# Mamba's softplus sums: from GpSimd additions to TensorE products with the identity

## The chip, the cores and the metric

The kernel runs on one core of one Trainium2 chip. The metric is the device time of one execution in microseconds (us). The core has five engines with a queue each: TensorE (matmuls, PE in the profile, its weight loads PEld), VectorE (DVE), ScalarE (ACT), GpSimd (POOL) and SyncE (SP), which here only issues transfers.

## The reference, cut to what matters

The network has four layers: two Mamba blocks, a convolution that makes local attention weights, linear attention with a mixture of experts, and softmax attention with a second mixture of experts. The change touches the Mamba blocks alone, all in float32, on 2 images of 1024 tokens with 256 channels (512 inside a block, 16 states):

```python
xs = jax.nn.silu(jnp.transpose(xc, (0, 2, 1)))          # after in_w and a causal convolution of 4 taps
x_dbl = xs @ xproj_w
dt, Bm, Cm = jnp.split(x_dbl, [DT_RANK, DT_RANK + D_STATE], axis=-1)
delta = jax.nn.softplus(dt @ dt_w + dt_b)
A = -jnp.exp(A_log)
dA = jnp.exp(delta[..., None] * A)
dBu = delta[..., None] * Bm[:, :, None, :] * xs[..., None]
def step(hst, ins):
    dA_t, dBu_t, C_t = ins
    hst = dA_t * hst + dBu_t
    y_t = jnp.einsum('bdn,bn->bd', hst, C_t)
    return (hst, y_t)
...
y = jnp.swapaxes(ys, 0, 1) + xs * Dp
y = y * jax.nn.silu(res)
out = y @ out_w + out_b
```

The kernel computes softplus(z) as max(z, 0) + ln(1 + e) with e = exp(-|z|). It corrects the logarithm for the rounding of 1 + e: with w = (1 + e) - 1 as rounded, it adds e - w. So delta is a sum of four terms, max(z, 0) + e + ln(1 + e) - w.

## The kernel before, in words

**Units.** Each Mamba block works through its 2048 tokens in 4 chunks of 512, so there are 8 units of one block and one chunk. The inner 512 channels are 4 parts of 128 (index dc), one channel to a partition, tokens along the free dimension. `layer0` (L575) runs the units one after the other. A unit has a front (`Mamba.front`, L293), a scan (`Mamba.scan`, L415) and a back (`Mamba.back`, L485).

**Front.** It makes xs (input projection L309, evicted by ScalarE at L313; convolution as 4 accumulating matmuls with diagonal matrices L336, evicted at L342; SiLU L345), then the small projection (L351), C transposed (L364), and z (L380). ScalarE takes from z's PSUM tile |z| into e (L385) and max(z, 0) into delta (L389), and runs exp (L393) and ln (L396) over all four parts at once. The tile e lies in the buffer tagged pre, which the next front's pre needs, and ln lies in the buffer tagged gate, which the back's gate needs (each tag has one buffer). Then for each of the four parts:

```python
nc.scalar.activation(w, e[:, dc, :], AF.Identity, bias=net.one)   # L403
nc.scalar.activation(w, w, AF.Identity, bias=net.minus_one)       # L404
eng.tensor_sub(w, e[:, dc, :], w)                                 # L405
eng.tensor_add(ln[:, dc, :], ln[:, dc, :], w)                     # L407
eng.tensor_add(delta[:, dc, :], delta[:, dc, :], ln[:, dc, :])    # L409
eng.tensor_mul(w, delta[:, dc, :], xs[:, dc, :])                  # L411, w is du
```

with a `yield` after each of the last four. The engine `eng` is GpSimd in seven units. The first unit's front runs alone, with no scan beside it (alone=True): there eng is VectorE, VectorE also does max(z, 0) (L387) and w (L401, one instruction), and exp and ln run part by part.

**Scan.** For each of 16 states n: a transfer spreads B's row over the partitions, GpSimd makes h = du * B for two parts at a time (L461; VectorE in the first state of the first unit), and for each of the 4 parts ScalarE makes da = exp(delta * A) in PSUM (L468, 3 buffers) and VectorE runs the recurrence (L472). So a unit has 64 scan steps. After each step two things advance by one: the work on the state before (TensorE transposes h for 128 tokens in four 128x128 pieces, L440, into one of 3 PSUM buffers; one step later VectorE multiplies by C and adds to ya, L449, or ScalarE does it for two of the states, L447), and `paced` (L552).

**Order of the work.** `paced` deals out generator steps over the 63 slots behind those scan steps by a table in `layer0`: for each generator a number of steps, a first slot and a last. Of the next unit's front, 22 steps (HEAD) go to slots 0 to 38, and 16 steps to slots 38 to 62. These 16 are the four yields of the four parts above. Beside them the back of the unit before has 9 steps in slots 0 to 35 (gate projection L494, evicted by ScalarE at L498 and put through SiLU at L502; y as L507 and transposes back L512, multiplied by the gate at L516) and 7 in slots 40 to 61 (output projection L524 and L528, layer norm L150 to L168, transposes L179, L540, and GpSimd's residual additions L543 and L548). The making of the next layer's taps (`Taps.make`: transposes L700, copies L702, matmuls L706, copies L711) has 9 steps, 12 in the first unit, in slots 40 to 63. All these matmuls share the two PSUM buffers tagged mm. Each engine runs its queue in order; the queues are laid down when the program is built and need not follow the order of the code.

**Diagonals.** GpSimd makes the convolution's diagonal matrices from the identity (L269), 128x128 each, before the first unit and again for the second block in slots 26 to 38 of the third.

Of the kernel before, what the change touches and what calls it, by code (L numbers as in the profile page):

```python
# [10 lines left out]
F32 = mybir.dt.float32  # L11
# [8 lines left out]
P = 128  # L20
# [7 lines left out]
TC = 512  # L28
# [205 lines left out]
class Mamba:  # L234
# [58 lines left out]
    def front(self, j, alone=False):  # L293


        net, nc, m, one, two = self.net, self.net.nc, self.m, self.one, self.two
        eng = nc.vector if alone else nc.gpsimd
# [3 lines left out]
        xs = two.tile([P, NDC, TC], F32, tag="xs", name=f"{m}_xs_{j}", bufs=3)  # L301
# [4 lines left out]
        for mc in range(NDC):  # L306
            ps = self.ps_mm.tile([P, TC], F32, tag="mm", name=f"{m}_in_{j}_{mc}")
            for kc in range(NCC):
                nc.tensor.matmul(  # L309
                    ps, lhsT=self.in_sb[:, kc, mc * P : (mc + 1) * P], rhs=self.xt[:, kc, tok],  # L310
                    start=(kc == 0), stop=(kc == NCC - 1),
# [8 lines left out]
        for dc in range(NDC):  # L320
            b = net.col(f"{m}_conv_b", dc)
# [12 lines left out]
            ps = self.ps_mm.tile([P, TC], F32, tag="mm", name=f"{m}_conv_{j}_{dc}")  # L334
            for k in range(4):
                nc.tensor.matmul(  # L336
                    ps, lhsT=self.taps[:, dc * 4 + k, :], rhs=pre[:, dc, k : k + TC],
                    start=(k == 0), stop=(k == 3),
# [10 lines left out]
        ps = self.ps_mm.tile([P, TC], F32, tag="mm", name=f"{m}_xd_ps_{j}")  # L349
        for dc in range(NDC):  # L350
            nc.tensor.matmul(  # L351
                ps[:XD, :], lhsT=self.xp_sb[:, dc, :], rhs=xs[:, dc, :],
                start=(dc == 0), stop=(dc == NDC - 1),
# [8 lines left out]
        ps = self.ps_mm.tile([P, TC], F32, tag="mm", name=f"{m}_ct_ps_{j}")  # L362
# [10 lines left out]
        delta = two.tile([P, NDC, TC], F32, tag="delta", name=f"{m}_delta_{j}")  # L373
        e = one.tile([P, NDC, 3 + TC], F32, tag="pre", name=f"{m}_e_{j}")[:, :, :TC]
        ln = one.tile([P, NDC, TC], F32, tag="gate", name=f"{m}_ln_{j}")
        du = two.tile([P, NDC, TC], F32, tag="du", name=f"{m}_du_{j}")
        for dc in range(NDC):
            pool, tag = (self.ps_ht, "ht") if alone and dc else (self.ps_mm, "mm")
            ps = pool.tile([P, TC], F32, tag=tag, name=f"{m}_dt_{j}_{dc}")
            nc.tensor.matmul(  # L380
                ps, lhsT=self.dt_sb[:, dc * P : (dc + 1) * P], rhs=xd[:RANK, :],
                start=True, stop=True,
            )
            b = net.col(f"{m}_dt_b", dc)
# [6 lines left out]
        parts = [slice(dc, dc + 1) for dc in range(NDC)] if alone else [slice(0, NDC)]  # L391
# [6 lines left out]
        for dc in range(NDC):  # L398
            w = du[:, dc, :]
            if alone:  # L400
                nc.vector.tensor_scalar(w, e[:, dc, :], 1.0, -1.0, ALU.add, ALU.add)  # L401
            else:
                nc.scalar.activation(w, e[:, dc, :], AF.Identity, bias=net.one)  # L403
                nc.scalar.activation(w, w, AF.Identity, bias=net.minus_one)  # L404
            eng.tensor_sub(w, e[:, dc, :], w)  # L405
            yield
            eng.tensor_add(ln[:, dc, :], ln[:, dc, :], w)  # L407
            yield
            eng.tensor_add(delta[:, dc, :], delta[:, dc, :], ln[:, dc, :])  # L409
            yield  # L410
            eng.tensor_mul(w, delta[:, dc, :], xs[:, dc, :])  # L411
            yield
        self.chunks[j] = xs, bd, ct, delta, du

# [137 lines left out]
def paced(n, parts):  # L552

    taken = [0] * len(parts)
    for slot in range(n):
        for i, (steps, many, first, end) in enumerate(parts):
            while taken[i] < many and slot >= first + (end - first) * taken[i] / many:
                next(steps, None)
                taken[i] += 1
        yield  # L560
    for steps, *_ in parts:
        for _ in steps:
            pass


def both(a, b, n):

    for i, _ in enumerate(a):
        if i % n == n - 1:
            next(b, None)  # L570
    for _ in b:
        pass


def layer0(net, x, x_dram, m1, m2, load_image, taps, conv_dram, lg):  # L575

    tc, nc = net.tc, net.nc  # L580
    with (
        tc.tile_pool(name="m_w", bufs=1) as wpool,
        tc.tile_pool(name="m_one", bufs=1) as one,
        tc.tile_pool(name="m_two", bufs=2) as two,
        tc.tile_pool(name="m_scan", bufs=2) as scanp,
        tc.tile_pool(name="m_dram", bufs=2, space=DRAM) as dram,
        tc.tile_pool(name="m_mm", bufs=2, space=PSUM) as ps_mm,
        tc.tile_pool(name="m_ht", bufs=3, space=PSUM) as ps_ht,
        ExitStack() as last,
    ):  # L590
        ps_da = last.enter_context(tc.tile_pool(name="m_da", bufs=3, space=PSUM))
        xt = x.rearrange("p c b t -> p c (b t)")
        pools = (wpool, one, two, scanp, dram, ps_mm, ps_da, ps_ht)
        blocks = [
            Mamba(net, "m1", pools, xt, None, *m1), Mamba(net, "m2", pools, xt, x_dram, *m2)
        ]
        norm = GroupNorm(net, wpool, ps_ht, x)
        blocks[0].load()
        for _ in blocks[0].diagonals():
            pass  # L600
        load_image()
        for _ in blocks[0].load_rest():
            pass
        rows = net.first_rows(wpool, ["m1_out_b", "m2_out_b"])
        for m, r in zip(blocks, rows):
            m.out_b = r
        norm.image(0)
        units = [(m, j) for m in blocks for j in range(NCH)]
        norm.image(1)
        for _ in units[0][0].front(0, alone=True):  # L610
            pass
        before, done = iter(()), []
        aside = taps.make(ps_mm, conv_dram)
        for u, (m, j) in enumerate(units):
            steps = [(b, Mamba.GATED, 0, 35) for b in done]
            fronts = []
            for a, k in units[u + 1 : u + 2]:
                if k == 0:
                    a.load()
                fronts.append(a.front(k))  # L620
            if u == NCH - 2:

                steps.append((blocks[1].diagonals(), NDC * 4, 26, 38))
            rest = m.load_rest() if u and j == 0 else iter(())
            steps += [(f, Mamba.HEAD, 0, 38) for f in fronts]
            steps += [(rest, 1, 37, 38)]
            steps += [(f, 16, 38, 62) for f in fronts] + [(b, 7, 40, 61) for b in done]
            steps += [(rest, 1, 62, 63)]
            if u + 1 < len(units):
                n = 9 if u else 12  # L630
                steps += [(islice(aside, n), n, 40, 63)]
            else:
                last.close()
                m.ps_da = last.enter_context(tc.tile_pool(name="m_da2", bufs=2, space=PSUM))
                ps_acc = last.enter_context(tc.tile_pool(name="m_acc", bufs=1, space=PSUM))

                def place(u):
                    pool, tag, w = {
                        3: (one, "pre", TC + 3), 0: (two, "xs", TC), 1: (two, "delta", TC),
                        2: (two, "du", TC),  # L640
                    }[u]
                    a = pool.tile(
                        [P, NDC, w], F32, tag=tag, name=f"early_{u}",
                        bufs=3 if tag == "xs" else None,
                    )
                    return taps.load(u, a.rearrange("p d t -> p (d t)"))

                pair = {u: place(u) for u in taps.ORDER}
                acc = {0: taps.bank(ps_acc.tile([P, TC], F32, tag="acc", name="early_acc"))}
                steps += [(taps.convolve(0, pair, acc), 56, 3, 63)]  # L650
            before = m.scan(j, before, paced(63, steps), u == 0)
            done = [m.back(j)]
        taps.read(acc, lg)
        for _ in before:
            pass
        acc = {
            k: taps.bank(ps_ht.tile([P, TC], F32, tag="ht", name=f"early_acc{k}")) for k in (1, 2)
        }
        both(taps.convolve(0, pair, acc), done[0], 3)
        taps.read(acc, lg)  # L660
# [945 lines left out]
def conv_attn_hybrid(ctx: ExitStack, tc: tile.TileContext, a: dict, out: bass.AP):  # L1606
# [6 lines left out]
    with tc.tile_pool(name="conv_w", bufs=2) as convw:  # L1613
        def load_x(b):
            for cc in range(NCC):
                nc.sync.dma_start(x[:, cc, b, :], a["x"][b, cc])

        load_x(0)
        taps = Taps(net, convw, main, x, a["l1_w1"], a["l1_w2"])
        layer0(  # L1620
            net, x, a["x"],
            [a[f"m1_{k}"] for k in ("in_w", "out_w", "xproj_w", "dt_w")],
            [a[f"m2_{k}"] for k in ("in_w", "out_w", "xproj_w", "dt_w")],
            lambda: load_x(1), taps, conv_dram, lg,
        )
# [117 lines left out]
```

## Time and profile before

| | us |
|---|---|
| runs of the kernel before | 2184.31, 2189.04, 2190.55 (median 2189.04) |
| the profiled execution's own time | 2188.29 |
| its span, first to last instruction | 2186.6 |
| Mamba stage, first scan to last scan | 53.3 to 1031 |
| TensorE busy, whole span | 1894.0 |
| VectorE busy, whole span | 1400.3 |
| GpSimd busy, whole span | 1028.9 |
| ScalarE busy, whole span | 959.2 |
| L405, L407, L409 on GpSimd, 28 of each | 33.2, 35.6, 35.6 |
| L472, 512 scans on VectorE | 318.7 + 303.3 |
| L449, 448 multiply-adds on VectorE | 320.2 |
| L461, 254 products on GpSimd | 594.5 |

How to read it: a view by stretch gives for each engine the time in which it was busy within a window. A view of waits gives, for an engine that stood idle, the instruction that then ran, the one whose end released it, and the sum, count and longest of such waits. In lines of groups the numbers after the count are busy time, mean ns of one, and idle time of the engine just before them with its releasers. In a timeline the columns are start, duration, engine, line, operation, tiles, shape and count, and in brackets the idle time before and its releaser; instructions of one kind that follow each other are one line. A float32 matmul appears as two MATMUL records, a transpose as one. A busy TensorE is not TensorE at its peak, since matmuls overlap and their ends are modelled. PEclk is the share of its full clock that TensorE was granted.

### The profile page before, as it was taken

What the parts mean: (1) busy time and instruction counts of PE and PEld (TensorE: products, weight loads), DVE (VectorE), ACT (ScalarE), POOL (GpSimd) and SP (SyncE); (2) the same over time, 40 slices, a digit from 0 to 9 for tenths busy, and PEclk for the clock granted to TensorE, in tenths of its full rate; (3) what the DMA queues carried; (4) which work ended last, traced back from release to release, by engine and by line L of the source; (5) the groups of instructions that cost most, each with busy time, mean ns of one, the idle gap of its engine ahead of it and who ended that gap; (6) DMA issues with size and microseconds to landing.
All of it is one profiled execution on the core that took longest, in us unless ns stands there. A gap on an engine that the chain in (4) does not pass through costs nothing.

```text
span 2186.6 us, 27311 instructions
## 1 busy us (share of the span) xinstructions
PE 1894.0 (87%) x9652; PEld 1335.5 (61%) x9652; DVE 1400.3 (64%) x2210; ACT 959.2 (44%) x1610; POOL 1028.9 (47%) x726
## 2 busy tenths in 40 slices
PE   6888898898978888788999989949999599859996
PEld 2464555556555655454646556539999467649995
DVE  6999998999999999899005475752222544432223
ACT  4676677767777767645013454411111132301111
POOL 3796787959698686965025420012332000023331
PEclk9869889898989889899999999969999799979997
DMA  2121121111212111310030100028998200059997
GB/s 106 45 68 39 37 69 35 58 35 45 62 47 60 38 49 35 85 42 17 0 64 1 48 15 10 20 82 306 326 329 323 82 10 10 20 206 327 329 323 292
DMA packets 90499, 223.87 MB, mean 102 GB/s; under 512 B 35467, under 2 KB 51728, under 8 KB 79732
## 3 DMA queue, kind: packets, MB, share of 16 engines
q1 hardware_dynamic: 77636, 198.29, 27.1%
q0 software_dynamic: 7728, 19.15, 2.9%
q10 hardware_dynamic: 4992, 4.59, 0.7%
q8 instruction: 81, 1.33, 0.3%
q14 instruction: 62, 0.51, 0.1%
HBM read 204.60 MB, written 19.37 MB: 102 GB/s over the span
## 4 chain that ended last, share of the span: by engine, by line
PE 32%; DVE 22%; issue 19%; POOL 11%; ACT 10%; DMA 5%; POOLq 0%; SPq 0%; DVEq 0%; ACTq 0%
DVE m_h L472 11%; DVE m_ya L449 6%; PE acc L762 3%; POOL x L1520 3%; POOL l_yd L1570 3%; PE m_ht L440 3%; PE early_acc L762 3%; PE av L1276 3%; ACT m_da L468 2%; PE sc L1250 2%; DMA l_yd<-y,target 2%; POOL m_h L461 2%; PE h L1099 2%; PE m_xd_ps L351 1%; PE w L1108 1%
## 5 line engine op out<-in xcount | busy, mean ns | idle before, releaser
L461 POOL TENSOR_TENSOR m_h<-m_du,m_b 128x1024 f32<-128x1024 f32 x254 | 594.5, 2364 | 196.0 <-PE m_ht L440 95.8
L440 PE MATMUL m_ht<-ident,m_h 128*128 128x128 f32 x2048 | 361.2, 305 | 119.4 <-DVE m_ya L449 83.9
L440 PEld LDWEIGHTS m_ht<-ident,m_h 128*128 128x128 f32 x2048 | 259.5, 154 | 317.8 <-DVE m_ya L449 112.7
L468 ACT ACTIVATE m_da<-m_delta,m_aneg 128x512 f32<-128x512 f32 x512 | 349.5, 690 | 220.8 <-DVE m_h L472 220.1
L1520 POOL DMA_INDIRECT x<-l_zd,source x82 | 84.8, 1034 | 573.1 <-DVE source L1465 217.1
L449 DVE SCALAR_TENSOR_TENSOR m_ya<-m_ht,m_ct,m_ya 128x512 f32<-128x512 f32 x448 | 320.2, 733 | 18.4 <-PE m_ht L440 17.5
L472 DVE TENSOR_TENSOR_SCAN m_h<-m_da,m_state,m_h 128x512 f32<-128x512 f32 x256 | 318.7, 1271 | 14.7 <-POOL m_h L461 8.7
L472 DVE TENSOR_TENSOR_SCAN m_h<-m_da,m_h 128x512 f32<-128x512 f32 x256 | 303.3, 1210 | 23.6 <-ACT m_da L468 13.1
L1550 PEld LDWEIGHTS h<-xts,we 128*128 128x128 f32 x2528 | 298.4, 194 | 7.1 <-issue 3.4
L1550 PE MATMUL h<-xts,we 128*128 128x128 f32 x2528 | 299.4, 277 | 2.2 <-issue 1.7
L1557 DVE TENSOR_TENSOR hid<-hid,h 128x512 f32<-128x512 f32 x79 | 54.3, 688 | 258.9 <-PE h L1550 258.9
L1556 ACT ACTIVATE hid<-h 128x512 f32<-128x512 f32 x79 | 47.2, 598 | 384.6 <-issue 324.0
L1564 PE MATMUL o<-we,hid 128*128 128x256 f32 x632 | 150.4, 380 | 2.2 <-DVE y L1569 1.6
L1570 POOL DMA_INDIRECT l_yd<-y,target x79 | 79.3, 1003 | 142.6 <-DVE y L1569 136.3
L1564 PEld LDWEIGHTS o<-we,hid 128*128 128x128 f32 x632 | 113.7, 190 | 15.7 <-DVE y L1569 2.8
L336 PE MATMUL m_conv<-m_pre,m_taps 128*128 128x512 f32 x240 | 114.6, 596 | 6.7 <-ACT m_gate L498 5.6
L762 PE MATMUL early_acc<-x,early 128*98 128x448 f32 (+21 forms) x308 | 97.0, 447 | 0.0
L762 PE MATMUL acc<-x,pair 128*98 128x416 f32 (+21 forms) x308 | 93.6, 452 | 0.0
L1569 DVE COPY y<-o 128x256 f32<-128x256 f32 x79 | 33.6, 425 | 69.6 <-PE o L1564 69.6
L309 PE MATMUL m_in<-x,m_in_sb 128*128 128x512 f32 x128 | 68.8, 663 | 9.8 <-ACT m_pre L313 6.9
L762 PEld LDWEIGHTS acc<-x,pair 128*98 128x98 f32 x308 | 47.7, 167 | 39.9 <-issue 34.5
L528 PE MATMUL m_out<-m_out_sb,m_xs 128*128 128x256 f32 x256 | 68.7, 397 | 0.0
(318 smaller groups left out, 2843.3 us busy)
## 6 DMA issues: line engine op xcount, KB each, us to landing
we<-in_l_experts_dram SPq DMA_DIRECT2D x82, 1536.0 KB
m_b<-m_bd SPq DMA_DIRECT2D x128, 256.0 KB
w<-in_l_w_dram SPq DMA_DIRECT2D x21, 256.0 KB
l_zd<-l_z SPq DMA_DIRECT2D x7, 512.0 KB
l_yl<-l_yd SPq DMA_DIRECT2D x10, 256.0 KB
l_yl<-l_yd ACTq DMA_DIRECT2D x10, 256.0 KB
early<-taps SPq DMA_DIRECT2D x7, 343.0 KB
pair<-taps SPq DMA_DIRECT2D x7, 343.0 KB
```

Source lines behind the costliest of these rows:

```text
L309: nc.tensor.matmul(ps, lhsT=self.in_sb[:, kc, mc * P : (mc + 1) * P], rhs=self.xt[:, kc, tok], start=(kc == 0), stop=(kc == NCC - 1),)
L336: nc.tensor.matmul(ps, lhsT=self.taps[:, dc * 4 + k, :], rhs=pre[:, dc, k : k + TC], start=(k == 0), stop=(k == 3),)
L440: nc.tensor.transpose(ps[:, dc * P : (dc + 1) * P], hs[dc // G][:, dc % G, i * P : (i + 1) * P], net.ident,)
L449: nc.vector.scalar_tensor_tensor(ya[:, i, :], ps, c, ya[:, i, :], ALU.mult, ALU.add)
L461: (nc.vector if start and n == 0 else nc.gpsimd).tensor_mul(h, du[:, g * G : (g + 1) * G, :], b.unsqueeze(1).to_broadcast(half))
L468: nc.scalar.activation(da, delta[:, dc, :], AF.Exp, scale=self.aneg[:, i : i + 1])
L472: nc.vector.tensor_tensor_scan(h, da, h, 0.0 if first else state[:, n, dc : dc + 1], ALU.mult, ALU.add)
L762: nc.tensor.matmul(a[:, lo - 16 * k : hi - 16 * k, co : co + n], lhsT=lhsT, rhs=self.x[:, kc, b, lo - r0 : hi - r0, ci : ci + n], start=(u ...
L1520: nc.gpsimd.indirect_dma_start(out=x, out_offset=None, in_=zd[:, :], in_offset=bass.IndirectOffsetOnAxis(ap=source[:, g : g + 1], axis=0), ...
L1550: nc.tensor.matmul(ps[:, at], lhsT=w12[:, s, kc, at], rhs=xt[:, kc * P : (kc + 1) * P], start=(kc == 0), stop=(kc == NCC - 1),)
L1564: nc.tensor.matmul(ps[:, :C], lhsT=ht[:, mc * P : (mc + 1) * P], rhs=w[:, 8 + mc, :], start=(mc == 0), stop=(mc == NHC - 1),)
L1570: nc.gpsimd.indirect_dma_start(out=yd[g], out_offset=bass.IndirectOffsetOnAxis(ap=target[:, g : g + 1], axis=0), in_=y, in_offset=None, bo ...
```

## The change

In each part, the three additions and subtractions (L405, L407, L409) give way to four accumulating matmuls: delta, e and ln each times the identity, and du (which holds w) times a new matrix, minus the identity. ScalarE copies the sum from PSUM to delta. The product with xs (L411) stays on eng; in the first unit's front it reads the sum from PSUM, elsewhere from delta. The sum lies in a buffer tagged mm; in the first unit's front the odd parts take one tagged ht. The yields of a part fall from four to three, and the table in `layer0` gives the front's second portion 12 steps in place of 16, over the same slots. GpSimd makes minus the identity once, ahead of the first unit.

```diff
@@ front, the loop over the four parts
             else:
                 nc.scalar.activation(w, e[:, dc, :], AF.Identity, bias=net.one)
                 nc.scalar.activation(w, w, AF.Identity, bias=net.minus_one)
-            eng.tensor_sub(w, e[:, dc, :], w)
-            yield
-            eng.tensor_add(ln[:, dc, :], ln[:, dc, :], w)
-            yield
-            eng.tensor_add(delta[:, dc, :], delta[:, dc, :], ln[:, dc, :])
-            yield
-            eng.tensor_mul(w, delta[:, dc, :], xs[:, dc, :])
+            yield
+
+            pool, tag = (self.ps_ht, "ht") if alone and dc % 2 else (self.ps_mm, "mm")
+            ps = pool.tile([P, TC], F32, tag=tag, name=f"{m}_sp_{j}_{dc}")
+            parts = (net.ident, delta), (net.ident, e), (net.ident, ln), (net.minus, du)
+            for k, (i, a) in enumerate(parts):
+                nc.tensor.matmul(
+                    ps, lhsT=i, rhs=a[:, dc, :], start=(k == 0), stop=(k == len(parts) - 1)
+                )
+            nc.scalar.copy(delta[:, dc, :], ps)
+            yield
+            eng.tensor_mul(w, ps if alone else delta[:, dc, :], xs[:, dc, :])
             yield
@@ layer0, before the units
+        net.minus = wpool.tile([P, P], F32, name="minus_ident")
+        nc.gpsimd.tensor_scalar_mul(net.minus, net.ident, -1.0)
@@ layer0, the table of a unit
-            steps += [(f, 16, 38, 62) for f in fronts] + [(b, 7, 40, 61) for b in done]
+            steps += [(f, 12, 38, 62) for f in fronts] + [(b, 7, 40, 61) for b in done]
```

## The prediction

> **What bounds the kernel now.** I read the busy time by stretch first. Counting 64 scans (L472) to a unit, a unit of the Mamba stage has an early part (scans 0 to 37, beside the next unit's projections) and a late part (38 to 63, where the softplus sums lie). Units 3 and 4, late, late and early, with the late part of unit 0 ahead:
>
> ```profile
> core 0: us, PE busy (x) PEld busy (x) DVE busy (x) ACT busy (x) POOL busy (x), PEclk, DMA share, GB/s
> 118.60:165.30 46.70, 39.92 (x180) 29.51 (x181) 43.91 (x49) 34.12 (x70) 45.30 (x29) 0.67 0.25 71
> 487.80:543.20 55.40, 44.63 (x231) 33.92 (x231) 50.25 (x63) 42.19 (x64) 50.10 (x31) 0.81 0.13 44
> 610.30:664.40 54.10, 42.43 (x230) 31.81 (x230) 49.63 (x65) 43.84 (x79) 50.69 (x33) 0.84 0.16 53
> 543.20:610.30 67.10, 62.22 (x286) 36.17 (x284) 65.19 (x74) 48.54 (x85) 48.30 (x24) 1.00 0.19 57
> ```
>
> VectorE is the bound: 97% busy early, 91% late, and its work is untouched by the change in seven of eight units. So at most its idle time can be won: 3 to 6 us in each late part, 33 us over seven (375.6 us of late parts less 342.8 busy). GpSimd is as busy as VectorE in the late part only; that is where its sums are. TensorE's clock is low there. Next, who VectorE waits for, from 118 to 914 us (us, times, longest):
>
> ```profile
> DVE m_h L472 <- ACT m_da L468: 19.0, 23, 2.5
> DVE m_h L472 <- POOL m_h L461: 17.3, 11, 4.9
> DVE m_ya L449 <- PE m_ht L440: 15.9, 22, 2.2
> ```
>
> Of the 17.3, the timeline puts 6.1 behind the tap diagonals of L269 and 2.7 behind residual adds and a DMA near 800 us; neither is touched. The other 8.5 lie at 165, 412, 419, 536, 664, 782 and 907 us: ends of late parts, or the first scan after one. GpSimd had lost its lead. Around 905 us, GpSimd and then ScalarE:
>
> ```profile
> 904.57 2.35 POOL L461 TENSOR_TENSOR m_h<-m_du,m_b 128x1024 f32<-128x1024 f32 x1
> 906.87 1.27 POOL L407 TENSOR_TENSOR m_ln<-m_ln,m_du 128x512 f32<-128x512 f32 x1
> 908.70 1.28 POOL L409 TENSOR_TENSOR m_delta<-m_delta,m_ln 128x512 f32<-128x512 f32 x1
> ```
> ```profile
> 910.01 0.69 ACT L498 ACTIVATE m_gate<-m_g,cols_sb 128x512 f32<-128x512 f32 x1 [6.57 <-POOL m_delta L409]
> ```
>
> The gate shares its buffer with ln, so ScalarE stood 6.57 us until GpSimd had added ln, and the exponentials (L468) behind it came late: VectorE lost 2.5 us at 911 and, the same way, 1.4 at 163.
>
> **What the Trainium skill says.** "Perfetto Trace Analysis", Identifying the Most-Contended Engine: matmul busy time does not measure headroom. The trace agrees: of the 44.63 us at 487.8, counted start to start at full clock (0.109 us for 128 columns, 0.216 for 256, 0.43 for 512), the records hold about 31 us, so TensorE has some 24 us to spare. "TensorE: Matmul & The Clock Gate", What's actually happening: an idle array runs at half clock until it has been busy for about a window of 3.4 us. The trace agrees: eight records in the time of four,
>
> ```profile
> 29.45 3.63 PE L351 MATMUL m_xd_ps<-m_xs,m_xp_sb 128*48 128x512 f32 x8
> ```
> ```profile
> 211.84 3.46 PE L351 MATMUL m_xd_ps<-m_xs,m_xp_sb 128*48 128x512 f32 x4
> ```
>
> and PEclk 0.67 to 0.84 late against 1.00 early. "SBUF — State Buffer", Who interferes with whom: a VectorE instruction with at most one SBUF input does not contend with GpSimd. The trace agrees: scans wholly under a GpSimd product took 1239 ns, scans beside none 1240. So fewer GpSimd instructions make no VectorE instruction of the scan faster.
>
> **The change, part by part.** Durations from groups by form:
>
> ```profile
> L405 POOL TENSOR_TENSOR m_du<-m_e,m_du 128x512 f32<-128x512 f32 x28 | 33.2, 1184 | 0.0
> L407 POOL TENSOR_TENSOR m_ln<-m_ln,m_du 128x512 f32<-128x512 f32 x28 | 35.6, 1273 | 1.1
> L409 POOL TENSOR_TENSOR m_delta<-m_delta,m_ln 128x512 f32<-128x512 f32 x28 | 35.6, 1271 | 1.5
> L336 PE MATMUL m_conv<-m_pre,m_taps 128*128 128x512 f32 x240 | 114.6, 596 | 6.7 <-ACT m_gate L498 5.6 <-ACT m_pre L313 1.1
> L702 ACT COPY w1ts<-w1t 128x512 f32<-128x512 f32 x21 | 12.3, 584 | 4.5 <-PE w1t L700 4.1 <-ACT m_state L432 0.2
> ```
>
> *Removed:* 84 GpSimd instructions, 33.2 + 35.6 + 35.6 = 104 us, 14.9 a unit: GpSimd falls from 50 to 35 us of a 54 us late part and keeps its lead. Worth the 8.5 us above; I add 1.5 of the 2.7 at 800 and the 1.9 just after 914, where adds fell on a lead already spent. Gain 10, bounds 8.5 and 13.1. *Moved:* ln is now released by TensorE, which does not queue behind products: the 2.5 + 1.4 = 3.9 us go.
>
> *Added, TensorE:* four matmuls a part. L336's 120 matmuls show as 240 records, two each, so 8 records x 0.43 = 3.44 us in one uninterrupted piece (6.9 at half clock), 13.8 a unit. 31 + 13.8 = 45 of 54 us: it fits. It also keeps the clock up: some 5 us of the 19.0 are late exponentials behind the tap copies, which wait for slow products late in the part (clock half from 519 to 536, 639 to 656, 765 to 782). I take half, 2.5; bounds 0 and 8 (with part of the m_ht waits). *Added, ScalarE:* 28 copies x 0.58 = 16 us, 2.3 a unit on 42 of 54 busy: hidden by its waits for scans. If that cover were gone, 16 us.
>
> *Added wait:* the copy waits for its four matmuls. Queued behind it are the exponentials that VectorE's next scans need, with three PSUM buffers of lead (one is used in 1.8 us: scan 1.14 and m_ya 0.64). GpSimd's product L411 waits for the copy, with the products of L461 behind it, but has 15 us of slack. The queues do not follow the program's order (at the start L405 runs at 38.5 us, before three earlier L387), so where a copy stands can't be read off the code. Bounds: below, what late hand-overs cost now, 5 us over some 66 in units 1 to 6, 0.07 each; above, a burst that outlasts the lead at half clock, 6.9 - 5.4 = 1.5. It can't be a gain, since it only adds a wait. The nearest bursts, L507 and L512 of the early part (0.86 + 16 x 0.11 = 2.6 us, four a unit), go with 1.7 us of waits in m_ht and 0.3 at L516 a unit, at most 0.5 each. I take 0.25: 28 x 0.25 = 7 us. Steps of the sums go from 16 to 12 over the same 24 slots, still six slots a part: nothing.
>
> *The first unit's front* runs alone, on VectorE, and is in the chain:
>
> ```profile
> 51.53 1.22 DVE L461 TENSOR_TENSOR m_h<-m_du,m_b 128x1024 f32<-128x1024 f32 x1
> 52.66 0.69 DVE L411 TENSOR_TENSOR m_du<-m_delta,m_xs 128x512 f32<-128x512 f32 x1
> 54.40 2.40 DVE L461 TENSOR_TENSOR m_h<-m_du,m_b 128x1024 f32<-128x1024 f32 x1
> 56.72 7.90 DVE L472 TENSOR_TENSOR_SCAN m_h<-m_da,m_h 128x512 f32<-128x512 f32 x7
> ```
>
> Twelve instructions x 0.6 = 7.3 us leave VectorE, but TensorE must do 16 matmuls = 13.8 us from about 38.2, some of it at half clock (+1.7): the fourth sum comes near 53.7, its product at 54.4, the second m_h (1.2 alone, 2.4 with GpSimd beside it) by 55.6 to 56.8, against 56.8 now. The saved 7.3 us turn into a wait for TensorE. Gain 1.5 by the middle of bounds: loss of 1 if no matmul runs ahead of the logarithms, gain of 3 at full clock. The new constant is one GpSimd instruction of 0.6 us while GpSimd idles (20 of the first 55 us busy): nothing, else 0.6. After unit 7 nothing changes.
>
> *Sum:* -10 - 3.9 - 2.5 - 1.5 + 7 = -10.9. The profiled execution took 2188.3 us (span 2186.6 and 1.7 around it), 0.75 below the median of the runs: 2188.3 - 10.9 = 2177.4. With all bounds good: 13.1 + 3.9 + 8 + 3 - 2 = 26 less, 2162. With the bad ones short of a burst that outlasts the lead (8.5 + 3.9 + 0 - 1 - 28 x 0.45 = -1.2): 2189.5.
>
> **The rivals.** *1, slower: the copy blocks the exponentials.* Place: ScalarE's queue in the late part. For it: late tap copies already wait up to 2.2 us for slow products, and these bursts are four times as long (6.9 against 8 x 0.21 = 1.7 at half clock). Against it: early parts hold 18 hand-overs of 0.9 to 1.7 us of matmuls with VectorE 97% busy. The gains are 17.9 us, so it decides from 17.9 / 28 = 0.64 us a burst on; at 1.5 it gives 2188.3 - 17.9 + 42 = 2212. *2, more is won:* with GpSimd free and the clock up, late parts run like early ones, VectorE 97% busy: 342.8 / 0.97 = 353 instead of 376, 22 less, with the start 3 and early waits 3: 2160. Against it: the late table loads of Exp and Ln stay, about 1 us a unit. *3, a swap:* waits for GpSimd become equal waits for ScalarE or TensorE, since VectorE's slack is small: 2187.
>
> **How the numbers follow.** Forecast 0.50 (2162 to 2190), rival 1 0.22, rival 2 0.20, rival 3 0.08. About 0.3% (6.6 us) is what a measurement of this kernel can tell from no change. Three quarters of the forecast and rival 2 are faster: 0.58; a quarter of the forecast and rival 3 are the same: 0.20; slower 0.22. The range runs from just below rival 2 to rival 1's price: 2158 to 2212.
>
> **What would show it.** GpSimd about 104 us less busy; no wait of VectorE for m_h at the ends of late parts; no wait of the gate for m_delta; PEclk in late parts up by a tenth; second m_h of the start by 57 us; VectorE's waits for m_da up by under 10 us. It is wrong if the late parts stay at 54 us or grow with m_da as their releaser (rivals 3 and 1), or if the start comes later than now.

## The result and the profile after

The kernel after took 2220.66 us (median of four runs, 2217.24 to 2224.36), against 2189.6 before, also of four: a ratio of 1.0147, 95% interval 1.0124 to 1.0171. The change makes the kernel 1.5% slower. The profiled execution took 2219.66 us with a span of 2218.0, 31.4 more than before. In the kernel after, the sum's matmuls are at L411, the copy at L414, the product with xs at L416, the transposes of h at L445, m_ya at L454, GpSimd's product h at L466, da at L473, the scan at L477, the output projection at L529 and L533, the making of taps at L708 to L719. From the page's first part:

```profile
PE 1960.2 (88%) x9908; PEld 1363.7 (61%) x9908; DVE 1398.0 (63%) x2198; ACT 975.4 (44%) x1642; POOL 925.6 (42%) x643
```

GpSimd lost 103.3 us of work, and VectorE has no more than it had. The same stretches as before, counted in scans again (unit 0 late, unit 3 late, unit 4 early, unit 4 late):

```profile
core 0: us, PE busy (x) PEld busy (x) DVE busy (x) ACT busy (x) POOL busy (x), PEclk, DMA share, GB/s
119.00:164.70 45.70, 38.70 (x196) 23.83 (x197) 43.23 (x49) 35.61 (x73) 34.56 (x19) 0.96 0.26 79
494.90:544.20 49.30, 43.62 (x198) 28.98 (x197) 48.09 (x61) 40.53 (x60) 32.77 (x15) 0.87 0.17 51
544.20:624.70 80.50, 74.48 (x340) 44.78 (x339) 67.88 (x77) 52.35 (x92) 50.75 (x26) 0.96 0.16 48
624.70:675.30 50.60, 44.03 (x209) 30.28 (x209) 47.85 (x61) 41.66 (x73) 33.99 (x18) 0.90 0.20 58
```

The late parts, where the change was made, are shorter: unit 3 by 6.1 us (55.4 to 49.3), with VectorE 98% busy. The early part behind it, which the diff does not touch, is 13.4 us longer (67.1 to 80.5), and VectorE stands idle in it for 12.6 us where it was 1.9. Over the whole Mamba stage, from the same cuts (us):

| stretch | before | after | difference |
|---|---|---|---|
| start, up to the first scan | 53.3 | 51.6 | -1.7 |
| late parts, units 0 to 6 | 375.6 | 343.7 | -31.9 |
| late part, unit 7 | 46.7 | 48.1 | +1.4 |
| early parts, units 0 and 1 | 137.4 | 135.6 | -1.8 |
| early parts, units 2 to 6 | 347.3 | 408.1 | +60.8 |
| early part, unit 7 | 70.8 | 73.7 | +2.9 |
| after the Mamba stage | 1155.3 | 1157.4 | +2.1 |

The rows add up to +31.8, the difference of the spans within rounding. So there is a gain of 32 us where the change lies, and a loss of 61 in five stretches that follow it. VectorE's waits from 118 to 914 us:

```profile
DVE m_h L477 <- POOL m_h L466: 35.3, 24, 5.5
DVE m_ya L454 <- PE m_ht L445: 33.6, 26, 4.0
DVE m_h L477 <- ACT m_da L473: 7.5, 13, 0.9
```

The wait for the exponentials (m_da), which the copy was feared to lengthen, fell from 19.0 to 7.5. Those for TensorE's transposes and for GpSimd's product doubled, and those that are new lie in early parts. The two waits together come to 64.5 us in the early parts of units 2 to 6, against 16.9 before. How they come about is seen at the end of unit 3. TensorE's timeline ("..." marks lines left out):

```profile
520.62 1.99 PE L533 MATMUL m_out<-m_out_sb,m_xs 128*128 128x256 f32 x8
...
523.72 1.99 PE L533 MATMUL m_out<-m_out_sb,m_xs 128*128 128x256 f32 x8
...
535.87 1.06 PE L708 MATMUL w1t<-ident,w 128*128 128x128 f32 x4
...
540.23 1.91 PE L411 MATMUL m_sp<-m_delta,ident 128*128 128x512 f32 x2
541.93 1.92 PE L411 MATMUL m_sp<-m_e,ident 128*128 128x512 f32 x2
543.64 1.48 PE L411 MATMUL m_sp<-m_ln,ident 128*128 128x512 f32 x2
544.95 1.02 PE L411 MATMUL m_sp<-m_du,minus_ident 128*128 128x512 f32 x2
...
548.50 1.12 PE L411 MATMUL m_sp<-m_delta,ident 128*128 128x512 f32 x2
549.47 1.02 PE L411 MATMUL m_sp<-m_e,ident 128*128 128x512 f32 x2
...
551.18 1.02 PE L411 MATMUL m_sp<-m_du,minus_ident 128*128 128x512 f32 x2
```

ScalarE in between:

```profile
533.11 1.93 ACT L168 ACTIVATE m_o<-m_out,ln_off,ln_rs 128x256 f32<-128x256 f32 x4 [0.21 <-DVE ln_off L166]
```

The output projection fills two PSUM tiles, one with its first matmul at 503.0, the other at 520.0, and these are the only two buffers tagged mm. Nothing frees them before the layer norm reads them at 533.1. From 525.7 to 535.87 TensorE has no matmul of that tag to do. Then everything that was held comes at once, at the seam between this late part and the next early part: tap products and their transposes, the unit's third sum (540.2 to 545.8; the granted clock was 0.5 until 544.5, and it is 1.7 us from one matmul to the next), the fourth sum (548.5 to 552), and the back's own transposes. The transposes of h stand in the same queue between these. VectorE and GpSimd at that time:

```profile
546.97 0.75 DVE L454 SCALAR_TENSOR_TENSOR m_ya<-m_ht,m_ct,m_ya 128x512 f32<-128x512 f32 x1 [1.59 <-PE m_ht L445]
...
552.79 0.75 DVE L454 SCALAR_TENSOR_TENSOR m_ya<-m_ht,m_ct,m_ya 128x512 f32<-128x512 f32 x1 [3.30 <-PE m_ht L445]
...
573.35 3.53 DVE L477 TENSOR_TENSOR_SCAN m_h<-m_da,m_h 128x512 f32<-128x512 f32 x3 [2.73 <-POOL m_h L466]
```
```profile
546.67 1.28 POOL L416 TENSOR_TENSOR m_du<-m_delta,m_xs 128x512 f32<-128x512 f32 x1 [8.53 <-ACT m_delta L414]
...
570.95 4.67 POOL L466 TENSOR_TENSOR m_h<-m_du,m_b 128x1024 f32<-128x1024 f32 x2 [3.86 <-PE m_ht L445]
```

VectorE waits 1.59 us behind the third sum and 3.30 behind the fourth. GpSimd stands 8.53 us for the third sum's copy, so it begins the new unit without a lead. The product that VectorE waits for at 573 (2.73 us) had itself stood 3.86 us until TensorE had transposed older h: there the wait for GpSimd is a wait for TensorE. The input projections of the next front, which began 1.6 us into the early part before (544.83), now begin 12.8 us into it (556.97). In the early part TensorE's busy time was already 62.22 of 67.1 us, so there is little room to catch up.

The order of TensorE's queue as built shows the crowding without any times. For unit 3, the work between one group of transposes of h and the next, at 0.43 us for each record of 512 columns (place 14.1 stands behind the transposes of h of state 14, second group of 128 tokens; it isn't a slot of the table in `layer0`):

```
before   output projection in 8.2 to 11.2, at most 1.3 us at one place
         nothing 11.3 to 13.1; taps and back's transposes 13.2 to 14.3, 0.4 to 1.2 us each
after    sums 0 and 1 with output projection 9.1 to 11.2, 2.1 to 4.7 us each
         nothing 11.3 to 13.2; 14.0: 4.53 (sum 2, taps)   14.1: 0.86   14.2: 3.87 (sum 3, transposes)
```

### The profile page after: what moved, and what is told of

It reads as the page before. It is cut to its first block, busy times and chain, and to the rows that moved or that the text cites. A ratio compares the mean times of both kernels' runs of the same rounds, so it can differ in the third digit from the quotient of the medians.

```text
span 2218.0 us, 27771 instructions
## 1 busy us (share of the span) xinstructions
PE 1960.2 (88%) x9908; PEld 1363.7 (61%) x9908; DVE 1398.0 (63%) x2198; ACT 975.4 (44%) x1642; POOL 925.6 (42%) x643
## 4 chain that ended last, share of the span: by engine, by line
PE 35%; DVE 21%; issue 19%; POOL 10%; ACT 10%; DMA 5%; POOLq 0%; SPq 0%; ACTq 0%; DVEq 0%
DVE m_h L477 11%; DVE m_ya L454 5%; POOL x L1528 3%; PE acc L770 3%; POOL l_yd L1578 3%; PE m_ht L445 3%; PE av L1284 3%; ACT m_da L473 2%; PE early_acc L770 2%; PE sc L1258 2%; DMA l_yd<-y,target 2%; PE m_sp L411 2%; PE h L1107 2%; POOL m_h L466 2%; PE m_xd_ps L351 1%
## 5 line engine op out<-in xcount | busy, mean ns | idle before, releaser
L466 POOL TENSOR_TENSOR m_h<-m_du,m_b 128x1024 f32<-128x1024 f32 x254 | 594.4, 2365 | 264.0 <-PE m_ht L445 145.9
L473 ACT ACTIVATE m_da<-m_delta,m_aneg 128x512 f32<-128x512 f32 x512 | 348.0, 690 | 217.2 <-DVE m_h L477 216.0
L445 PEld LDWEIGHTS m_ht<-ident,m_h 128*128 128x128 f32 x2048 | 247.0, 147 | 247.7 <-DVE m_ya L454 100.4
L445 PE MATMUL m_ht<-ident,m_h 128*128 128x128 f32 x2048 | 318.2, 288 | 88.0 <-DVE m_ya L454 70.9
L454 DVE SCALAR_TENSOR_TENSOR m_ya<-m_ht,m_ct,m_ya 128x512 f32<-128x512 f32 x448 | 316.5, 732 | 35.6 <-PE m_ht L445 34.5
L477 DVE TENSOR_TENSOR_SCAN m_h<-m_da,m_state,m_h 128x512 f32<-128x512 f32 x256 | 316.2, 1267 | 17.9 <-POOL m_h L466 12.1
L477 DVE TENSOR_TENSOR_SCAN m_h<-m_da,m_h 128x512 f32<-128x512 f32 x256 | 301.3, 1207 | 29.2 <-POOL m_h L466 24.7
L499 PE MATMUL m_g<-x,m_gate_sb 128*128 128x512 f32 x128 | 66.7, 640 | 1.2 <-ACT m_pre L313 1.1
```

The costliest lines, as they stand in the source:

```text
L445: nc.tensor.transpose(ps[:, dc * P : (dc + 1) * P], hs[dc // G][:, dc % G, i * P : (i + 1) * P], net.ident,)
L454: nc.vector.scalar_tensor_tensor(ya[:, i, :], ps, c, ya[:, i, :], ALU.mult, ALU.add)
L466: (nc.vector if start and n == 0 else nc.gpsimd).tensor_mul(h, du[:, g * G : (g + 1) * G, :], b.unsqueeze(1).to_broadcast(half))
L473: nc.scalar.activation(da, delta[:, dc, :], AF.Exp, scale=self.aneg[:, i : i + 1])
L477: nc.vector.tensor_tensor_scan(h, da, h, 0.0 if first else state[:, n, dc : dc + 1], ALU.mult, ALU.add)
L499: nc.tensor.matmul(ps, lhsT=self.gate_sb[:, kc, dc * P : (dc + 1) * P], rhs=xt[:, kc, tok], start=(kc == 0), stop=(kc == NCC - 1),)
```

## The experiments

The theory, A: the two mm buffers, held by the output projection, press half of the unit's sums together with the rest of the mm work at the seam of late and early part; TensorE's queue is full there, the transposes of h come late, and the early part cannot make it up. Its form A1 lays the loss on the lateness of the sums (GpSimd waits for delta, the next front for the buffer of e), A2 on the amount of TensorE work packed at that place. Against A stood rival 1 of the prediction (the copy holds up the exponentials on ScalarE), and theory B: the sums are simply too much for TensorE wherever they stand. Ratios are to the kernel before, with 95% intervals. "Early 2 to 6" is the sum of those five early parts, 347.3 us before and 408.1 after.

**The output projection evicted at once, in the kernel after and, as a control, in the kernel before.**

```diff
-            found.append(a)
+            if i % 2:
+                nc.scalar.copy(o[:, i - 1 : i + 1, :].rearrange("p a c -> p (a c)"), ps)
...
-        net.norm_rows(tiles, found, nc.scalar)
+        net.norm_rows(tiles, tiles, nc.scalar)
```

> The changed kernel, but the back copies each pair of output projections out of PSUM by ScalarE at once (2 copies of 128x512 a unit) and the layer norm reads the copy, so that the projection no longer holds both buffers tagged mm until its norm is done. Theory A (the two mm buffers are held by the output projection for some 10 slots, so two of the four sums are pushed together at the end of the late part and the next early part starts late): the third sum moves into the middle of the late part, waits for m_ht at the start of units 2 to 7 fall, early parts of units 2 to 6 come back from 79-83 us to 70-73, time about 2165 us (2155 to 2185). Theory B (TensorE has too much work with 13.8 us a unit more, wherever it stands): early parts stay at 79 to 83 us, time 2212 to 2225.

> The kernel before with the same copy of the output projections. Control for the first run: theory A expects little, since nothing but the tap steps waits for the mm buffers there: 2178 to 2195 us. Theory B expects the same.

Measured: 2175.49 us, 0.9948 [0.9930, 0.9966], for the first: by the ratios 44 us less than the change, and faster than the kernel before. The control: 2181.67, 0.9980 [0.9973, 0.9987]. Early 2 to 6: 352.8. In the first, unit 3's third sum starts at 519.18 and its fourth at 532.13, 13 us apart, where they were 8 apart; in the queue the third has moved from 14.0 to 12.1. The window of unit 4's early part, with the columns as above, and VectorE's waits:

```profile
537.90:606.50 68.60, 64.07 (x298) 38.40 (x298) 65.84 (x75) 48.76 (x87) 47.54 (x23) 0.98 0.16 50
```
```profile
DVE m_h L477 <- ACT m_da L473: 13.9, 23, 1.0
DVE m_h L477 <- POOL m_h L466: 10.8, 9, 5.5
DVE m_ya L454 <- PE m_ht L445: 9.9, 18, 1.2
```

The early part is back at 68.6 us, and the waits for transposes and for GpSimd are below those of before (15.9 and 17.3). The control gains 0.2%, so the freed buffers are worth 4 us by themselves and 44 with the sums; with buffers freed on both sides the sums win 6 us (2181.67 to 2175.49). So the loss comes with the held buffers. Whether it is by lateness or by crowding is not told apart here. The late parts of units 0 to 6 sum to 360.6 us, 15 less than before the change and 17 more than with it: about half of what the change gained in its late parts goes again, presumably because the work no longer slides out of them.

**A PSUM buffer for the sums alone.** PSUM is full, so it is taken from the exponentials, and the kernel before with two buffers for them is the yardstick.

```diff
-        ps_da = last.enter_context(tc.tile_pool(name="m_da", bufs=3, space=PSUM))
+        ps_da = last.enter_context(tc.tile_pool(name="m_da", bufs=2, space=PSUM))
+        ps_sp = last.enter_context(tc.tile_pool(name="m_sp", bufs=1, space=PSUM))
...
-            pool, tag = (self.ps_ht, "ht") if alone and dc % 2 else (self.ps_mm, "mm")
+            pool, tag = (self.ps_ht, "ht") if alone and dc % 2 else (self.ps_mm, "mm") if alone else (self.ps_sp, "sp")
```

> The changed kernel with a PSUM buffer of its own for the sums of the seven fronts that run beside a scan, paid for by one of the three buffers of the exponentials (2 instead of 3). Theory A: the sums leave the mm buffers, none is pushed to the end; early parts of units 2 to 6 at 70 to 73 us, time about 2165 us plus what the lost buffer costs (fourth run). Theory B: early parts stay at 79 us and more, time 2212 us or more.

> The kernel before with two buffers of the exponentials instead of three: the price of the buffer alone. Both theories: 0 to 25 us more than before, since ScalarE's lead over VectorE falls from three steps to two.

Measured: 2185.7 us, 1.0006 [0.9995, 1.0018], for the sums with their own buffer; 2215.63, 1.0142 [1.0117, 1.0168], for the yardstick (30 us, a little more than the 0 to 25 expected). Early 2 to 6: 358.8, in the yardstick 355.2. Freed from the mm buffers the sums win 30 us against a kernel with the same two buffers for exponentials; in the queue of unit 3 the third sum then stands at 12.1 and the fourth at 13.1 to 13.3. That supports A by another way, at the price of a buffer that is worth as much itself.

**The sums of the first unit's front alone,** with the GpSimd operations kept in the seven others and the table back at 16 steps.

```diff
-            nc.scalar.copy(delta[:, dc, :], ps)
-            eng.tensor_mul(w, ps if alone else delta[:, dc, :], xs[:, dc, :])
+            if alone:
+                ...
+                nc.scalar.copy(delta[:, dc, :], ps)
+                eng.tensor_mul(w, ps, xs[:, dc, :])
+                yield
+                continue
+            eng.tensor_sub(w, e[:, dc, :], w)
...
```

> Only the first unit's front takes its sums on TensorE; the seven fronts beside a scan keep the GpSimd sums and the 16 steps. It times the start by itself. The first scan came 1.7 us earlier in the changed kernel (51.6 against 53.3 us). Both theories: 1 to 3 us less than before, about 2184 us, and late and early parts as before.

Measured: 2187.05 us, 1.0005 [0.9992, 1.0019]: the 1 to 3 us expected are not there; the start brings nothing that can be measured.

**The sums ahead of the output projection,** by the table alone.

```diff
-            steps += [(f, 12, 38, 62) for f in fronts] + [(b, 7, 40, 61) for b in done]
+            steps += [(f, 12, 38, 50) for f in fronts] + [(b, 7, 50, 62) for b in done]
```

> The changed kernel with another table: the 12 steps of the sums in slots 38 to 50, the 7 steps of the back in slots 50 to 62. All four sums then come before the output projection takes the mm buffers. If it matters where the sums stand (a narrow form of theory A: the sums' own lateness), the loss goes: about 2170 us. If what matters is that the projection holds both mm buffers until its norm (theory A as I hold it), the hold now ends in the next early part and stops that unit's gate and input projections instead: 2195 to 2225 us, with the loss at the first slots of units 2 to 7. Theory B: 2212 us or more, spread over the early parts.

Measured: 2206.8 us, 1.0114 [1.0084, 1.0144]. Early 2 to 6: 368.3, 40 us less than with the change; but late parts of 54 to 59 us in units 1 to 6, and waits for m_da of 27.4, for m_h 23.3. In unit 3 the sums now stand at 8.2 to 11.1, and the output projection at 11.3 to 13.1; the gate and input projections of the new unit bunch behind them, 8.6 us between two groups of transposes (555.5 to 564.5). That is what theory A expected in its wider form. The sums themselves are early here: the fourth product with xs ends 22 us or more before the next unit's first scan, and a loss of 21 us in the early parts stays. The loss moves with the place of the packed work.

**Shorter bursts:** the first experiment with each sum in two steps of two matmuls, 16 steps in all.

```diff
+                if k == 1:
+                    yield
...
+            steps += [(f, 16, 38, 62) for f in fronts] + [(b, 7, 40, 61) for b in done]
```

> The changed kernel with the projections copied out (as in the first experiment) and the four matmuls of a sum in two steps of two, with 16 steps over the same slots as before the change. If bursts of 3.44 us still cost VectorE something, it falls: 2165 to 2172 us. If they don't, 2171 to 2178 us as in the first experiment.

Measured: 2177.69 us, 0.9966 [0.9954, 0.9978], with an interval that overlaps the unsplit one's. Shorter bursts and 16 steps, changed together, win nothing.

**More TensorE work:** the first experiment with six matmuls a sum (e added and taken off again).

```diff
+            if not alone:
+                parts = ((net.ident, e), (net.minus, e)) + parts
```

> The changed kernel with the projections copied out and six matmuls for each of the 28 sums beside a scan (e is added and taken off once more): 48 us more of TensorE, bursts of 5.2 us in place of 3.44. It prices the burst. Theory A (TensorE has room in the late part once the mm buffers are free): 0 to 0.5 us a sum, 2175 to 2190 us. Theory B (any more TensorE work lands on the path): 30 to 48 us more, 2205 to 2223 us.

Measured: 2208.93 us, 1.0112 [1.0090, 1.0134]: 1.6% or some 35 us more than with four, for 28 x 2 x 0.86 = 48 us of matmuls, with waits for transposes at 36.5. That lies in theory B's range (2205 to 2223) and outside theory A's: even well spread, TensorE has little room beyond the four. GpSimd waits 64.3 us for the copies of the sums here, more than the 55.2 with the change, while early 2 to 6 sum to 365.3, 43 less: this wait's total by itself doesn't make the loss.

**Less TensorE work at the same late place:** the kernel after with one matmul a sum in the seven units beside a scan. It leaves out e, ln and w, so delta there is max(z, 0) alone.

```diff
+            parts = parts if alone else parts[:1]
```

> The changed kernel with one matmul in place of four for each of the 28 sums beside a scan (it leaves out e, the logarithm and w there, so delta is max(z, 0)): the same number of mm buffers taken, the same copies by ScalarE, a quarter of TensorE's work (10.3 us a unit less). Theory A1 (the held mm buffers themselves make the last two sums too late for the next scan): the loss stays, 2205 to 2220 us. Theory A2 (the held buffers only press TensorE's work together at the end of the late part, 8.4 us in two slots, and that work delays the transposes): the loss goes, 2165 to 2185 us.

Measured: 2180.82 us, 0.9978 [0.9969, 0.9987]; early 2 to 6: 346.4, as before the change. The mm buffers are still held by the output projection here, delta is still copied from PSUM, and the last two sums stand at 13.3 and 14.1 of unit 3's queue, one place ahead of those with the change (14.0 and 14.2). So the held buffers and the late place alone do not cost. This speaks against A1 as it was put, but does not part lateness from crowding: with less work the sums are also done sooner. In units 1 to 6 the fourth product with xs (L417) ends between 4.6 us before the next unit's first scan and 1.1 after it; with the change it ends 3.9 to 10.0 us after. These sums also no longer wait for e, ln and w, nor hold their buffers.

**The same cuts with the output evicted:** one matmul (the same terms left out), and three, with the subtraction e - w back on GpSimd.

```diff
+            parts = parts if alone else parts[:1]
```
```diff
+                eng.tensor_sub(w, e[:, dc, :], w)
...
+            parts = (net.ident, delta), (net.ident, ln), (net.ident, e) if alone else (net.ident, du)
```

> The same one matmul a sum, with the output projections copied out as in the first experiment. If the four matmuls of 3.44 us still cost something there (six cost 33 us more than four), one gives 2155 to 2168 us; if four fit into TensorE's idle time, 2171 to 2178 us as with four.

> The changed kernel with the projections copied out, and e - w taken by GpSimd again (L405), so that a sum beside a scan is three matmuls, 2.58 us: 24 us less TensorE, 33 us more GpSimd than the first experiment. If TensorE's load is what is left of the cost there, 2165 to 2173 us, the best of the kernels that compute everything; if GpSimd's lead is worth as much, 2173 to 2180 us.

Measured: 2184.96 us, 0.9992 [0.9977, 1.0006], and 2191.37, 1.0025 [1.0010, 1.0039]. Both miss: with less TensorE work than the first experiment they are slower than it. Their early parts are short (345.1 and 343.2 for units 2 to 6); their late parts in units 1 to 6 are 53 to 57 us, and the waits for exponentials are 30.8 and 28.4 us, against 13.9. That is rival 1's place. Which instruction ahead of the exponentials does it was not found: each edit may also move the copies in ScalarE's queue. This stays open. It limits what can be claimed: less TensorE work is not by itself more speed.

**The harm without the change:** the kernel before, with four matmuls ahead of each of the back's two groups of transposes in one PSUM tile, which the transposes then overwrite; no new buffer, copy or wait.

```diff
-            ps = net.transposed(self.ps_mm, tiles, cc, "mm")
+            ps = self.ps_mm.tile([P, TC], F32, tag="mm", name=f"mm_t_{j}_{cc}")
+            for k in range(4):
+                nc.tensor.matmul(ps, lhsT=net.ident, rhs=y[:, cc, :], start=True, stop=True)
+            for i, a in enumerate(tiles):
+                nc.tensor.transpose(
+                    ps[:, i * P : (i + 1) * P], a[:, cc * P : (cc + 1) * P], net.ident
+                )
```

> The kernel before, GpSimd sums and all, with nothing added but TensorE work where the change packs it: ahead of each of the back's two groups of transposes (L179) four matmuls of 512 columns into the same PSUM buffer, which the transposes then overwrite, 6.9 us a unit at about slots 60 and 61. No buffer, copy or wait is added. Theory A2 (TensorE's work pressed together at the end of the late part is the harm): waits for m_ht and then m_h in the first slots of units 2 to 7 as in the changed kernel, early parts at 76 to 83 us, 2210 to 2250 us. If the harm comes from the sums themselves (late delta and du, or ScalarE's copies), 2184 to 2200 us.

Measured: 2245.66 us, 1.0272 [1.0253, 1.0291], 61 us more; early 2 to 6: 390.8. Of the 59.7 us between the two profiled spans 43.5 lie in these five early parts, and 14 after the Mamba stage. Its waits, and the window of unit 4's early part:

```profile
DVE m_h L472 <- POOL m_h L461: 43.2, 28, 5.2
DVE m_ya L449 <- PE m_ht L440: 31.2, 34, 3.5
```
```profile
561.60:637.70 76.10, 69.10 (x315) 41.06 (x313) 66.43 (x73) 49.33 (x87) 48.35 (x24) 0.98 0.17 50
```

The picture is that of the change: VectorE waits for GpSimd's product and for transposes, and unit 4's early part is 9 us longer than before, with 9.7 us of idle time (76.10 - 66.43). The added matmuls are 8 x 0.86 = 6.9 us a unit, as two sums are. No sum is late here: the fourth product with xs ends 2.3 us before the next unit's first scan, as before (2.4 to 4.0), and GpSimd and VectorE still wait for TensorE. So TensorE work at the seam is enough for a loss of 43.5 us where the change lost 60.8. Whether the other 17 come of the late sums is open; no run has late sums without packed work.

## Why the prediction was wrong

**The step that failed** is "31 + 13.8 = 45 of 54 us: it fits". The records of a late part do hold that little, but the sum was made over the part as a whole. The sums could not stand anywhere in it: they need an mm buffer, and the output projection holds both from its second tile until the layer norm. Two of four sums, with the taps and the back's transposes that need the same buffers, were left for the end: 4.53 + 0.86 + 3.87 = 9.3 us of work at three neighbouring places of the queue. What this step priced at nothing cost 61 us in the early parts of units 2 to 6. The signs of being wrong that the prediction named, late parts and the start, did not show it, since the loss lies behind them. Nor were the "some 24 us to spare" free where buffers allow: with the buffers freed, 48 us more of matmuls cost some 35. Unit 1 shows the other side: the late part ahead of it, unit 0's, has no output projection, since no unit lies before it. Its last three sums start at 128.69, 140.84 and 149.52, spread over a part that ends at 164.7, and the early part that follows became shorter, from 72.1 to 68.2 us.

**GpSimd's slack.** That L411 "waits for the copy, with the products of L461 behind it, but has 15 us of slack" failed with it. GpSimd's waits from 118 to 914 us:

```profile
POOL m_h L466 <- PE m_ht L445: 113.8, 29, 6.8
POOL m_du L416 <- ACT m_delta L414: 55.2, 13, 9.0
```

The new wait is 55.2 us in 13 pieces, up to 9.0, and the products of h stand behind it. The 15 us of work were saved, but the free time came as waits at the seam and gave no lead there. How much of the loss this wait makes by itself is the open part above; the larger one is for TensorE's transposes, 113.8 us against 81.5 before.

**Right:** GpSimd's work (104 forecast, 103.3 measured); no wait of VectorE for its product at the ends of late parts; no wait of the gate for delta; the clock in late parts rose (0.67, 0.81 and 0.84 to 0.96, 0.87 and 0.90), in two of these three by less than the tenth forecast; twelve steps for sixteen (nothing, as far as the split bursts, which change both, can show).

**Right in direction, wrong in size:** the late parts of units 0 to 6 gained 32 us where the steps that lie in them summed to -10 - 3.9 - 2.5 + 7 = -9.4. Rival 2's mechanism fits there (VectorE 98% busy in unit 3's late part), and its 22 was still low. But with the output projection evicted at once the same parts gain 15, so part of the 32 is probably work that slid into the early parts. The copies' 7 us were not seen in the change: the wait for exponentials fell by 11.5. That price is not refuted in general, since three other arrangements (sums first, one matmul, three matmuls) have waits of 27 to 31 us there.

**The start** was forecast well in its parts but not in its sum. The fourth sum ends at 53.96 (forecast 53.7). VectorE then:

```profile
55.23 0.69 DVE L416 TENSOR_TENSOR m_du<-m_sp,m_xs 128x512 f32<-128x512 f32 x1 [0.75 <-ACT m_delta L414]
...
57.10 5.67 DVE L477 TENSOR_TENSOR_SCAN m_h<-m_da,m_h 128x512 f32<-128x512 f32 x5
```

The product reads the sum from PSUM, yet waits for ScalarE's copy of it. The Trainium skill, "PSUM — Partial Sum Buffer", PSUM bank collisions raise a hardware error, says that two engines must not be on one bank at once, readers included, so the two readers go in turn; the trace agrees, with 0.75 us of idle time that the copy's end closes. The first scan came 1.7 us earlier, but the eighth ends at 64.65 against 64.62 before: the gain of 1.5 us was none.

**Rival 1,** which came nearest in time (2212), had the wrong mechanism: the wait that took the place of the removed ones is for TensorE and, through it, for GpSimd.

## What to carry to other kernels

Room on an engine must be looked for where the buffers let the work stand: for each PSUM buffer that the new work shares, follow who holds it from its first write to its last read. When a change makes an untouched stretch longer, read what is queued ahead of it on the busiest engine at the seam. A cheap early eviction can be worth more than the change that needs it: two copies of 0.58 us a unit turned a ratio of 1.0147 into 0.9948.

## What the runs showed of the hardware

- A float32 matmul of 512 columns is two records, 0.43 us apart at full clock and 0.85 at half (549.47 to 551.18 and 540.23 to 543.64 in the kernel after, four records each), so an estimate of 3.4 or 6.8 us for a sum of four.
- 6.9 us of TensorE work at a full seam cost 43.5 us in the five early parts of units 2 to 6, 8.7 each: more than the work itself.
- One of three PSUM buffers for the exponentials is worth 1.42% (some 30 us) in this kernel, although an exponential takes 0.69 us and a scan with its m_ya 1.8.
